# A graph layer's expert stage: results scattered in pairs of rows by node, second biases inside the products, and the full group's work between the other groups' gates

## The chip, the cores and the metric

The kernel runs on one core of a Trainium2 chip. The metric is device time in microseconds (us) of one execution; a comparison uses the median of several. A core has TensorE (PE in the profile; its weight loads are PEld), VectorE (DVE), ScalarE (ACT), GpSimd (POOL) and SyncE (SP), which mostly issues DMAs here. POOL issues the indirect DMAs, in which each of 128 partitions names the row of DRAM that it reads or writes.

## The reference

There are 3125 nodes with 512 features and 53125 edges. Two layers of graph attention and a mixing branch come first; they fill most of the time and don't change. What changes is the last step, a mixture of experts on the layer-normalized rows:

```python
logits = xf @ Wg + bg                       # 8 experts
probs = jax.nn.softmax(logits, axis=-1)
_, top_idx = jax.lax.top_k(probs, 2)
mask = jnp.any(top_idx[:, :, None] == jnp.arange(8)[None, None, :], axis=1)
comb = probs * mask.astype(probs.dtype)
for e in range(8):
    h = jax.nn.gelu(xf @ W1[e] + b1[e])     # 512 -> 128
    y = h @ W2[e] + b2[e]                   # 128 -> 512
    out = out + comb[:, e:e + 1] * y
```

The weights of the two chosen experts are not divided by their sum. All is float32.

## The kernel before

Nodes are sorted by degree and cut into 25 tiles of 128 rows (the last has 53), which stand in seven groups of four (the last has one tile). The features of a group lie transposed in SBUF as `xT`. A list scheduler orders the instructions of each engine; each engine then runs its own list strictly in that order, waiting where a semaphore says so. The tail of the program, `last`, works in stages.

**Gates** (`gates`, `in_turn`). Per group there are three passes over its tiles: transpose back to rows (L1050) and take row statistics; scale and add to `yall`, the running result (L1061, L1063), with statistics again; then normalize to `z` on ACT (L1074), store `z` to the DRAM table `zld` (L1078, on SP), transpose `z` (`to_features`, L463) and multiply with the gate weights (L1082). `in_turn` runs up to three groups at once, one pass apart. The rows of `yall` are gathered and added by POOL, tile by tile (L994, L997), the tile of 53 rows first and the full group's tiles last.

**One group is treated in full.** The tiles of group 5 (tiles 20 to 23, `ALL_EXPERTS`) go through all eight experts (`all_experts`: first products L1169, ACT's Gelu L1172, second products L1176, additions on DVE L1178). The other 21 tiles are **listed**: `choose` finds each node's two experts, `lists` sorts the node-expert pairs into 48 **parts** of 128 places, each part of one expert, and makes `which`, the rows of `zld` that a part reads, and `placei`, the two places of each node.

**Parts** (`one_expert`). POOL gathers 128 rows of `zld` (L1281), PE transposes them, multiplies with the first weights (L1288) and adds the first bias by a product of three bf16 rows (L1290: the bias cut into three bf16 pieces, against ones), ACT applies Gelu, PE transposes (L1297) and multiplies with the second weights (L1300), DVE copies (L1302), and SP stores the result to `yld` (L1303), in the order of places.

**Order of the stages.** The gates of the listed groups run first; then the first biases' bf16 rows are made (`first_biases`: POOL L1152, L1153, SP L1154, L1155); then `choose` and `lists`, with the full group's gates beside them; the full group's `second_biases` (L1139: weights of the experts, transposed, times the eight rows of biases; L1141 adds) and four of its experts' steps; the 48 parts; the other four steps. At the end, per listed tile: the second biases, two gathers from `yld` by place (L1334), two weighted additions (L1337) and a scatter to the output by node (`put`, L1158).

Buffers that matter: PSUM tags `tr` (two), `ph` (two), `py` (three) and `pg` (one); SBUF `z` (three) and `yt` (five).

Of the kernel before, what the change touches and what calls it, by code (L numbers as in the profile page):

```python
# [9 lines left out]
F32 = mybir.dt.float32  # L10
BF16 = mybir.dt.bfloat16
I32 = mybir.dt.int32
AF = mybir.ActivationFunctionType
OP = mybir.AluOpType
# [3 lines left out]
N = 3125  # L18
D = 512
# [8 lines left out]
NX = 8  # L28
# [390 lines left out]
def listed_layers(ctx: ExitStack, tc: tile.TileContext, rows,  # L419
# [581 lines left out]
    def last(xT, w1t, w2t, b2t, wgt, bgt, gt, b1t, yall):  # L1001
        with tc.tile_pool(name="fin", bufs=1, reuse_waits="tile") as fp, \
                tc.tile_pool(name="fin_p", bufs=2, space=PSUM, reuse_waits="tile") as pp:

            zld = tc.dram_tile([(NL - 1) * P + LISTED[-1][1], D], F32, name="zld")
            yld = tc.dram_tile([PARTS * P, D], F32, name="yld")

# [16 lines left out]
                           allow_small_or_imprecise_dtypes=True)  # L1024
            tiles_at = fp.tile([P, NL], F32, name="tiles_at")
            nc.gpsimd.iota(tiles_at, pattern=[[1, NL]], base=0, channel_multiplier=0,
                           allow_small_or_imprecise_dtypes=True)
            puts = []

            def gates(t0, k):  # L1030
# [6 lines left out]
                if listed:  # L1037
                    u0 = LISTED.index(tiles[0])
                    prob, rank = lprob[:, u0:u0 + k, :], lrank[:, u0:u0 + k, :]
                else:  # L1040
                    prob = fp.tile([P, GT, NX], F32, name="prob", bufs=2)
                    rank = fp.tile([P, GT, NX], F32, name="rank")
                nc.vector.memset(mv, 1.0)
                nc.vector.memset(mv2, 1.0)
                nc.vector.memset(prob, 0.0)
                yt = []
# [25 lines left out]
                for i, (t, n) in enumerate(tiles):  # L1072
                    z = fp.tile([P, D], F32, name="z", bufs=3)
                    nc.scalar.activation(z[:n], yall[:n, t, :], AF.Identity,  # L1074
                                         bias=mv2[:n, i, 0:1], scale=sd[:n, i:i + 1])
                    if listed:
                        r = (u0 + i) * P
                        nc.sync.dma_start(zld[r:r + n, :], z[:n])  # L1078
                    to_features(pp, "py", xT[:, :, t * P:t * P + n], z, n, nc.scalar.copy, bufs=3)
                    pg = pp.tile([P, NX], F32, name="pg", tag="ph", bufs=2)  # L1080
                    for c in range(NP):
                        nc.tensor.matmul(pg[:n], lhsT=xT[:, c, t * P:t * P + n], rhs=wgt[:, c, :],  # L1082
                                         start=(c == 0), stop=(c == NP - 1))
                    nc.vector.tensor_add(prob[:n, i, :], pg[:n], bgt[:n])
                    yield prob[:, :k, :], rank[:, :k, :]

            def in_turn(groups):

                running, groups, said = [], list(groups), None
                while running or groups:  # L1090
                    if groups:
                        running.append([gates(*groups[0]), groups.pop(0)[1]])

                    for i in range(GT):
                        for r in reversed(running):
                            if i < r[1]:
                                said = next(r[0])
                    for r in list(running):
                        r.append(None)
                        if len(r) == 5:  # L1100
                            running.remove(r)
                return said

# [38 lines left out]

            def first_biases():

                b1p = pp.tile([NX, FX], F32, name="b1p", tag="pg", bufs=1)
                nc.tensor.transpose(b1p, colt[:, XB1:XB1 + NX], ident)
                left = fp.tile([NX, FX], F32, name="left")
                nc.scalar.copy(left, b1p)
                b1s = fp.tile([NX, 3, FX], BF16, name="b1s")
                b1d = tc.dram_tile([NX, 3, FX], BF16, name="b1d")  # L1150
                for i in range(3):
                    nc.gpsimd.tensor_copy(b1s[:, i, :], left)  # L1152
                    nc.gpsimd.tensor_sub(left, left, b1s[:, i, :])  # L1153
                nc.sync.dma_start(b1d, b1s)  # L1154
                nc.sync.dma_start(b1t, b1d.rearrange("e i f -> i e f"))  # L1155

            def put(t, n):
                puts.append(nc.gpsimd.indirect_dma_start(  # L1158
                    out=out, out_offset=bass.IndirectOffsetOnAxis(ap=node(t), axis=0),
                    in_=yall[:n, t, :], in_offset=None))  # L1160

            def all_experts(t0, k, prob):

                gs = slice(t0 * P, min(N, (t0 + k) * P))
                w = gs.stop - gs.start
                for e in range(NX):
                    ph = pp.tile([FX, 512], F32, name="ph", bufs=2)
                    for c in range(NP):
                        nc.tensor.matmul(ph[:, :w], lhsT=w1t[:, e, c, :], rhs=xT[:, c, gs],  # L1169
                                         start=(c == 0), stop=(c == NP - 1))  # L1170
                    hT = fp.tile([FX, GT * P], F32, name="hT", tag="yt", bufs=5)
                    nc.scalar.activation(hT[:, :w], ph[:, :w], AF.Gelu_apprx_tanh,  # L1172
                                         bias=colt[:, XB1 + e:XB1 + e + 1])
                    for i, (t, n) in enumerate(TILES[t0:t0 + k]):
                        py = pp.tile([P, 512], F32, name="py", bufs=3)
                        nc.tensor.matmul(py[:n], lhsT=hT[:, i * P:i * P + n], rhs=w2t[:, e, :],  # L1176
                                         start=True, stop=True)
# [6 lines left out]
            def lists():  # L1184
# [45 lines left out]
                for o, values in ((place, both), (weight, lprob)):  # L1230
                    for i in range(2):
# [14 lines left out]
                                  for i in (0, 2, 1))  # L1246
# [5 lines left out]
                nc.scalar.activation(hots[:, :, 0, :], hot, AF.Copy, scale=number[:, 0:1])  # L1252
                nc.vector.tensor_tensor(hots[:, :, 1, :].rearrange("p (u i) q -> p u i q", i=2),
                                        hot.rearrange("p (u i) q -> p u i q", i=2),
                                        tiles_at[:, :, None, None].to_broadcast([P, NL, 2, PARTS]),
                                        OP.mult)
                pw = pp.tile([P, 2, PARTS], F32, name="pw", tag="pg", bufs=1)
                for j in range(2 * NL):
# [6 lines left out]
                nc.vector.tensor_copy(whichf, pw)  # L1265
                nc.vector.scalar_tensor_tensor(which, whichf[:, 1, :], float(P), whichf[:, 0, :],
                                               op0=OP.mult, op1=OP.add)
# [7 lines left out]
                nc.vector.tensor_copy(experti, expert)  # L1275
                return placei, weight, which, experti

            def one_expert(part, e, which):

# [19 lines left out]
                py = pp.tile([P, 512], F32, name="py", bufs=3)  # L1299
                nc.tensor.matmul(py, lhsT=h1T, rhs=w2t[:, bass.ds(e, 1), :], start=True, stop=True)  # L1300
                y1 = fp.tile([P, D], F32, name="y1", tag="z", bufs=3)
                nc.vector.tensor_copy(y1, py)  # L1302
                nc.sync.dma_start(yld[part * P:(part + 1) * P, :], y1)  # L1303


            in_turn(g for g in FGROUPS[-1:] + FGROUPS[:-1] if g not in ALL_EXPERTS)
            first_biases()
            choose(lprob, lrank)
            placei, weight, which, experti = lists()
            work = []  # L1310
            for g in ALL_EXPERTS:
                prob, rank = in_turn([g])
                choose(prob, rank)
                second_biases(*g, prob)
                work.append(all_experts(*g, prob))
            work = chain(*work)
            for _ in range(4):
                next(work)
            RB = 8
            for p0 in range(0, PARTS, RB):  # L1320
# [3 lines left out]
                for i, e in enumerate(es):  # L1324
                    one_expert(p0 + i, e, which)
            for _ in work:
                pass
            for u, (t, n) in enumerate(LISTED):
                if u % GT == 0:
                    k = min(GT, NL - u)  # L1330
                    second_biases(t, k, lprob[:, u:u + k, :])
                for i in range(2):
                    y1 = xT.tiles[4 if i else 2][:, u % 4, :]
                    nc.gpsimd.indirect_dma_start(  # L1334
                        out=y1[:n], out_offset=None, in_=yld[:, :],
                        in_offset=bass.IndirectOffsetOnAxis(ap=placei[:n, u, i:i + 1], axis=0))
                    nc.vector.scalar_tensor_tensor(yall[:n, t, :], y1[:n], weight[:n, u, i:i + 1],  # L1337
                                                   yall[:n, t, :], op0=OP.mult, op1=OP.add)
                put(t, n)
# [619 lines left out]
```

## Time and profile before

| | us |
|---|---|
| three runs: median (lowest to highest) | 2759.18 (2756.99 to 2768.11) |
| the profiled execution: time | 2757.61 |
| its span | 2755.9 |
| PE busy | 2279.7 (83%) |
| DVE busy | 1989.4 (72%) |
| POOL busy | 1482.9 (54%) |
| ACT busy | 1398.9 (51%) |
| 906 gathers of the attention (L592) on POOL | 1120.2 |
| last function, from the first gate work to the end | 2326.3 to 2755.9 |

The profile is of one execution. A row of a group gives line, engine, operation, tiles, count, busy time, mean duration in ns, and the idle time of the engine just before with what ended it. Timeline rows begin with start and duration in us. Shares of busy time are averages over stages with different limits, so the stages are read one by one. PEclk is the clock that TensorE was granted, as a share of full speed. A float32 product appears as two passes, so `x8` is four products.

### The profile page before, as it was taken

The page shows a single profiled execution, that of the slowest core. Times are in us where ns is not written, and L with a number is a line of the kernel's source. Part 1 is how long each engine was busy: PE and PEld are TensorE (multiplying, and loading weights), DVE is VectorE, ACT ScalarE, POOL GpSimd, SP SyncE. Part 2 cuts the span into 40 slices and gives each one's busy share as a digit, 9 for nine tenths or more (in the row PEclk, how much of TensorE's full clock was granted, in tenths as well). Part 3 has the DMA queues.
Part 4 walks back from the last instruction along what each step waited for, and adds up shares of the span by engine and source line. Part 5 has one row for each costly group of instructions (what it writes and reads, how often), then busy time and mean ns, then how long its engine had stood idle before and what let it go on. Part 6 is the DMA issues. An engine that isn't in the chain of part 4 may idle for free. (4 is left out here: it accounts for less than half of the span.)

```text
span 2755.9 us, 31740 instructions
## 1 busy us (share of the span) xinstructions
PE 2279.7 (83%) x9030; PEld 1302.4 (47%) x9030; DVE 1989.4 (72%) x3067; ACT 1398.9 (51%) x5365; POOL 1482.9 (54%) x1254
## 2 busy tenths in 40 slices
PE   6987988889889886999698778979897667679983
PEld 3442445555455544444344445555555343656731
DVE  6820889999999995601578988989898658664354
ACT  1111568788777773300185768776766533432200
POOL 3361778877777771011456665656667438102346
PEclk9998999989999997999799898889898868569985
DMA  8433999999989984331678878888988564214644
GB/s 283 178 118 127 341 324 330 330 338 328 338 321 344 340 308 149 131 117 76 239 253 299 317 283 314 305 321 309 320 320 285 187 185 141 71 43 124 189 132 150
DMA packets 232307, 661.88 MB, mean 240 GB/s; under 512 B 51442, under 2 KB 56951, under 8 KB 228024
## 3 DMA queue, kind: packets, MB, share of 16 engines
q0 software_dynamic: 169632, 541.48, 56.4%
q1 hardware_dynamic: 59937, 113.31, 11.3%
q10 hardware_dynamic: 2556, 4.97, 0.5%
q8 instruction: 77, 1.26, 0.2%
q14 instruction: 105, 0.86, 0.1%
HBM read 567.10 MB, written 92.69 MB: 239 GB/s over the span
## 5 line engine op out<-in xcount | busy, mean ns | idle before, releaser
L592 POOL DMA_INDIRECT lane<-kvd,idx x906 | 1120.2, 1236 | 543.0 <-issue 192.1
L633 ACT ACTIVATE lane<-lane,sc 128x64 f32<-128x64 f32 x3888 | 945.4, 339 | 113.3 <-DVE sc L623 112.9
L597 DVE TENSOR_TENSOR lane<-lane,q 128x1024 f32<-128x1024 f32 (+1 forms) x464 | 548.8, 1193 | 152.7 <-DMA lane<-kvd,idx 149.1
L653 PE MATMUL agg<-ident,lane 128*128 128x128 f32 (+1 forms) x3272 | 529.0, 301 | 139.9 <-DVE lane L636 59.4
L653 PEld LDWEIGHTS agg<-ident,lane 128*128 128x128 f32 (+1 forms) x3272 | 422.6, 154 | 314.8 <-ACT lane L633 139.5
L598 DVE TENSOR_REDUCE sc<-lane 128x16 f32<-128x1024 f32 (+1 forms) x464 | 545.3, 1187 | 2.7 <-ACT lane L633 1.7
L636 DVE TENSOR_TENSOR lane<-lane,sc 128x1024 f32<-128x1024 f32 (+1 forms) x214 | 252.3, 1197 | 0.1
L564 PE MATMUL pq<-wq,xg 128*128 128x512 f32 (+1 forms) x400 | 200.9, 632 | 17.9 <-ACT kt L743 8.5
L710 PE MATMUL po<-aT,wo 128*128 128x512 f32 (+1 forms) x448 | 198.7, 585 | 20.1 <-ACT aT L697 12.1
L1281 POOL DMA_INDIRECT xT<-zld,which x48 | 45.4, 946 | 218.5 <-DVE more L1120 116.7
L503 POOL DMA_INDIRECT kvd<-kv,rec x25 | 24.5, 980 | 223.7 <-DVE kv L500 217.7
L710 PEld LDWEIGHTS po<-aT,wo 128*128 128x128 f32 x448 | 83.3, 211 | 97.3 <-issue 65.0
L500 DVE COPY kv<-pv 128x512 f32<-128x512 f32 (+1 forms) x25 | 17.3, 692 | 153.1 <-PE pv L497 153.1
L564 PEld LDWEIGHTS pq<-wq,xg 128*128 128x128 f32 (+1 forms) x400 | 73.3, 199 | 93.5 <-issue 69.2
L381 ACT COPY kv<-pkv 128x512 f32<-128x512 f32 (+1 forms) x50 | 29.1, 585 | 163.7 <-PE pkv L379 140.1
L379 PE MATMUL pkv<-wk,xT 128*128 128x512 f32 (+1 forms) x200 | 100.7, 637 | 5.7 <-ACT kv L381 5.7
L729 PE MATMUL pq<-wmk,zT 128*128 128x512 f32 (+1 forms) x200 | 99.6, 617 | 5.6 <-ACT kt L743 3.4
L729 PE MATMUL pq<-wmp,mqT 128*128 128x512 f32 (+1 forms) x200 | 98.0, 632 | 5.3 <-ACT mqT L852 4.8
L729 PE MATMUL pq<-wmv,zT 128*128 128x512 f32 (+1 forms) x200 | 99.5, 614 | 3.2 <-DVE vt L782 2.5
L743 ACT ACTIVATE mq<-pq,hm 128x64 f32<-128x64 f32 (+1 forms) x200 | 59.3, 320 | 70.5 <-DVE hm L740 70.4
L379 PE MATMUL pkv<-wv,xT 128*128 128x512 f32 (+1 forms) x200 | 92.3, 603 | 0.0
L729 PE MATMUL pq<-wmq,zT 128*128 128x512 f32 (+1 forms) x200 | 91.4, 595 | 0.0
(339 smaller groups left out, 3275.3 us busy)
## 6 DMA issues: line engine op xcount, KB each, us to landing
lane<-kvd,idx POOLq DMA_INDIRECT x906, 6.3
kvd<-kv SPq DMA_DIRECT2D x24, 512.0 KB, 2.7
zT<-ztd SPq DMA_DIRECT2D x48, 256.0 KB, 5.9
yld<-y SPq DMA_DIRECT2D x48, 256.0 KB, 2.0
xmid<-xg SPq DMA_DIRECT2D x10, 1024.0 KB, 5.7
xT<-xmid POOLq DMA_DIRECT2D x10, 1024.0 KB, 9.5
xr<-in_x SPq DMA_DIRECT2D x24, 256.0 KB, 3.8
xb<-xo SPq DMA_DIRECT2D x24, 256.0 KB, 5.7
```

What stands on the lines that cost most here:

```text
L379: nc.tensor.matmul(ps[:n], lhsT=xT[t][:, c, :n], rhs=wkv[name][:, c, :], start=(c == 0), stop=(c == NP - 1))
L564: nc.tensor.matmul(ps[:n], lhsT=of_place(t, c), rhs=wq[:, c, :], start=(c == 0), stop=False)
L592: gets.append(nc.gpsimd.indirect_dma_start(out=kv[:n, k, :], out_offset=None, in_=kvd[l][:, :], in_offset=bass.IndirectOffsetOnAxis(ap=idx ...
L597: nc.vector.tensor_mul(ks, ks, self.q[:n, None, :].to_broadcast([n, g, D]))
L598: nc.vector.tensor_reduce(self.sc[:n, :, j:j + g].rearrange("p h g -> p g h"), ks.rearrange("p g (h d) -> p g h d", h=H), AX.X, OP.add)
L633: nc.scalar.activation(v[:, k, h, :], v[:, k, h, :], AF.Copy, scale=self.sc[:n, h, j + k:j + k + 1])
L636: nc.vector.tensor_mul(v, v, self.sc[:n, :, j:j + g].rearrange("p h g -> p g h")[:, :, :, None] .to_broadcast([n, g, H, DH]))
L653: nc.tensor.matmul(self.agg[:, c * n:(c + 1) * n], lhsT=kv[:n, k, c * 128:(c + 1) * 128], rhs=ident[:n, :n], is_transpose=True, start=firs ...
L710: nc.tensor.matmul(ps[:, :w], lhsT=wo[:, kk, c * 128:(c + 1) * 128], rhs=aT[gi][:, kk, :w], start=(kk == 0), stop=(kk == NP - 1))
L729: nc.tensor.matmul(ps[:n], lhsT=lhs(c), rhs=w[:, c, :], start=(c == 0), stop=(c == NP - 1 and bias is None))
L743: nc.scalar.activation(oh[:, h, :], ph[:, h, :], AF.Exp, bias=m[:n, h:h + 1], accum_out=s[:n, h:h + 1])
L1281: nc.gpsimd.indirect_dma_start(out=x1, out_offset=None, in_=zld[:, :], in_offset=bass.IndirectOffsetOnAxis(ap=which[:, part:part + 1], axi ...
```

## The change

- **Second biases.** `b2` is cut into three bf16 pieces as `b1` was (`biases`: three POOL copies, two subtractions, three stores and one load on SP), and each part's second product gets one more product of three rows (ones times the pieces). `second_biases` is left for the full group alone.
- **Scatter in pairs.** The result of a part goes to `yld` by an indirect DMA on POOL, to row 2 x node + choice (`goes`; places without a node go to rows of their own). A listed tile then reads both results of its nodes by one direct load on SP of 4 KB a partition. `lists` gets some small DVE steps that make `which` and `goes`.
- **Order.** The full group runs second in `in_turn`; then its `choose`, `second_biases` and one step of its experts a turn, between the gates of the other groups. What is left of the steps comes behind `lists` in the program. The order that the scheduler makes of it puts 32 of 32 first and 21 of 32 second products ahead of the last gate product.
- **Gates.** The products of a group's tiles share one PSUM buffer and one addition of the bias; the biases' bf16 rows are made behind the gates. The experts' hidden values of the full group lie in the last tile's free columns instead of a `yt` buffer.

```diff
-            zld = tc.dram_tile([(NL - 1) * P + LISTED[-1][1], D], F32, name="zld")
-            yld = tc.dram_tile([PARTS * P, D], F32, name="yld")
+            zld = tc.dram_tile([NL * P + LISTED[-1][1], D], F32, name="zld")
+            VOID = 2 * P * (NL + 1)
+            yld = tc.dram_tile([VOID + PARTS * P, D], F32, name="yld")
...
-                        r = (u0 + i) * P
+                        r = (u0 + i + 1) * P
                         nc.sync.dma_start(zld[r:r + n, :], z[:n])
+                        if u0 + i == 0:
+                            nc.sync.dma_start(zld[:n, :], z[:n])
                     to_features(pp, "py", xT[:, :, t * P:t * P + n], z, n, nc.scalar.copy, bufs=3)
-                    pg = pp.tile([P, NX], F32, name="pg", tag="ph", bufs=2)
+                    if i == 0:
+                        pg = pp.tile([P, GT, NX], F32, name="pg", bufs=1)
                     for c in range(NP):
...
-                    nc.vector.tensor_add(prob[:n, i, :], pg[:n], bgt[:n])
+                    if i == k - 1:
+                        if n < P:
+                            nc.vector.memset(prob, 0.0)
+                        nc.vector.tensor_add(prob[:n, :k, :], pg[:n, :k, :],
+                                             bgt[:n, None, :].to_broadcast([n, k, NX]))
...
+                            if r[2] in ALL_EXPERTS:
+                                prob, rank = said
+                                choose(prob, rank)
+                                second_biases(*r[2], prob)
+                                beside.append(all_experts(*r[2], prob))
+                    if beside:
+                        next(beside[0], None)
...
+                b2d = tc.dram_tile([NX, 3, D], BF16, name="b2d")
+                left = b2t
+                for i in range(3):
+                    b2p = fp.tile([P, D], F32, name="b2p", tag="yt", bufs=5)
+                    part = b2p.bitcast(BF16)[:NX, :D]
+                    nc.gpsimd.tensor_copy(part, left)
+                    nc.sync.dma_start(b2d[:, i, :], part)
+                    if i < 2:
+                        rest = fp.tile([P, D], F32, name="rest", tag="yt", bufs=5)[:NX]
+                        nc.gpsimd.tensor_sub(rest, left, part)
+                        left = rest
...
-                    hT = fp.tile([FX, GT * P], F32, name="hT", tag="yt", bufs=5)
+                    r0 = P + e % 2 * P
+                    hT = xT.tiles[-1][:, :, r0:r0 + P]
...
+                both_at = fp.tile([P, 2, PARTS], I32, name="both_at")
+                nc.vector.tensor_copy(both_at[:, 0, :], whichf[:, 1, :])
+                nc.vector.tensor_scalar(both_at[:, 1, :], both_at[:, 0, :], 1, None, op0=OP.bitwise_and)
+                nc.vector.tensor_scalar(both_at[:, 0, :], both_at[:, 0, :], 1, None,
+                                        op0=OP.logical_shift_right)
...
-                nc.tensor.matmul(py, lhsT=h1T, rhs=w2t[:, bass.ds(e, 1), :], start=True, stop=True)
+                nc.tensor.matmul(py, lhsT=h1T, rhs=w2t[:, bass.ds(e, 1), :], start=True, stop=False)
+                nc.tensor.matmul(py, lhsT=one[:, :P], rhs=b2s[:, bass.ds(e, 1), :],
+                                 start=False, stop=True)
                 y1 = fp.tile([P, D], F32, name="y1", tag="z", bufs=3)
                 nc.vector.tensor_copy(y1, py)
-                nc.sync.dma_start(yld[part * P:(part + 1) * P, :], y1)
+                results.append(nc.gpsimd.indirect_dma_start(
+                    out=yld[:, :], out_offset=bass.IndirectOffsetOnAxis(ap=goes[:, part:part + 1], axis=0),
+                    in_=y1, in_offset=None))
-            in_turn(g for g in FGROUPS[-1:] + FGROUPS[:-1] if g not in ALL_EXPERTS)
-            first_biases()
+            work = []
+            in_turn(FGROUPS[-1:] + ALL_EXPERTS + [g for g in FGROUPS[:-1] if g not in ALL_EXPERTS],
+                    work)
+            b2s = biases()
             choose(lprob, lrank)
-            placei, weight, which, experti = lists()
-            work = []
-            for g in ALL_EXPERTS:
-                prob, rank = in_turn([g])
-                choose(prob, rank)
-                second_biases(*g, prob)
-                work.append(all_experts(*g, prob))
-            work = chain(*work)
-            for _ in range(4):
-                next(work)
+            weight, which, goes, experti = lists()
+            for _ in work[0]:
+                pass
...
             for u, (t, n) in enumerate(LISTED):
-                if u % GT == 0:
-                    k = min(GT, NL - u)
-                    second_biases(t, k, lprob[:, u:u + k, :])
+                y2 = xT.tiles[(2, 0, 4)[u // 2 % 3]][:, u % 2 * 2:u % 2 * 2 + 2, :]
+                r = 2 * P * (u + 1)
+                nc.sync.dma_start(y2[:n], yld[r:r + 2 * n, :].rearrange("(r i) d -> r i d", i=2))
                 for i in range(2):
-                    y1 = xT.tiles[4 if i else 2][:, u % 4, :]
-                    nc.gpsimd.indirect_dma_start(
-                        out=y1[:n], out_offset=None, in_=yld[:, :],
-                        in_offset=bass.IndirectOffsetOnAxis(ap=placei[:n, u, i:i + 1], axis=0))
-                    nc.vector.scalar_tensor_tensor(yall[:n, t, :], y1[:n], weight[:n, u, i:i + 1],
+                    nc.vector.scalar_tensor_tensor(yall[:n, t, :], y2[:n, i, :], weight[:n, u, i:i + 1],
                                                    yall[:n, t, :], op0=OP.mult, op1=OP.add)
                 put(t, n)
```

## The prediction

> **What bounds the kernel now.** I read the chain of waits first: its pieces after 2326 us are nearly all of the last function, so I cut the profiled execution (span 2755.9, time 2757.61, so 1.7 lie around it; the median of the three runs is 2759.18, 1.6 more) into stages by busy time in windows: gates, choice and lists, a start of the experts, the experts' 48 parts, the end.
>
> ```profile
> core 0: us, PE busy (x) PEld busy (x) DVE busy (x) ACT busy (x) POOL busy (x), PEclk, DMA share, GB/s
> 2326.30:2429.30 103.00, 70.37 (x344) 63.07 (x344) 70.55 (x205) 45.18 (x82) 24.68 (x29) 0.55 0.25 82
> 2429.30:2470.50 41.20, 29.43 (x126) 19.20 (x126) 33.81 (x148) 14.98 (x19) 0.01 (x1) 0.67 0.00 1
> 2470.50:2498.70 28.20, 24.72 (x53) 10.35 (x53) 16.49 (x36) 1.86 (x3) 5.70 (x6) 0.82 0.19 56
> 2498.70:2634.90 136.20, 136.20 (x768) 96.17 (x767) 45.79 (x98) 38.01 (x94) 39.68 (x42) 1.00 0.57 173
> 2634.90:2755.90 121.00, 65.14 (x122) 23.91 (x120) 59.09 (x85) 2.75 (x4) 72.11 (x67) 0.62 0.46 145
> ```
>
> Three different limits. The gates: no engine is over 70%, the TensorE clock is granted at 0.55. The 48 parts: TensorE without a gap, 136.2/48 = 2.8 us each. The end: POOL, by the groups of 2665 to 2745:
>
> ```profile
> L1334 POOL DMA_INDIRECT xT<-yld,placei x34 | 36.7, 1080 | 10.4 <-issue 10.4
> L1337 DVE SCALAR_TENSOR_TENSOR yall<-xT,weight,yall 128x512 f32<-128x512 f32 (+1 forms) x41 | 29.9, 748 | 24.7 <-DMA xT<-yld,placei 24.5
> L1158 POOL DMA_INDIRECT out<-yall,rec x20 | 22.2, 1111 | 6.9 <-issue 4.3 <-DVE yall L1337 2.0 <-DMA out<-yall,rec 0.3
> ```
>
> POOL is busy 59 of 80 us and most of its idle time is the 0.3 us between two issues: 42 gathers and 21 puts at some 1.4 us are the end.
>
> Then the clock, from the timeline of PE in the gates and behind them:
>
> ```profile
> 2375.35 1.91 PE L463 MATMUL tr<-ident,z 128*128 128x128 f32 x8
> 2378.77 0.96 PE L1082 MATMUL pg<-wgt,xT 128*128 128x8 f32 x8
> 2411.01 3.42 PE L1082 MATMUL pg<-wgt,xT 128*128 128x8 f32 x16
> 2451.29 9.57 PE L1169 MATMUL ph<-xg,w1t 128*128 128x512 f32 x16
> 2476.22 6.72 PE L1139 MATMUL pb<-b2t,combT 8*128 8x512 f32 x8
> 2482.87 16.02 PE L1176 MATMUL py<-w2t,hT 128*128 128x512 f32 x32
> ```
>
> A tile's gate product takes 1.71 at half clock (16 passes in 3.42) and 0.96 at full. The 512-wide passes take 0.86 at half and 0.44 at full: 9.57 for 16 is a start at half and a rise after some 5 us. The second biases (8 rows) stay at half clock through 6.72 us.
>
> **The change part by part.**
>
> *Gates, +40.* The changed program's order on PE puts between the full group's last gate product and the last gate product of all: 32 first and 21 second expert products (106 passes) and 4 bias products (8 passes); 11 second products come behind. 106 x 0.44 = 47, 8 x 0.84 = 7, and some 4 us for two starts at half clock: +57 or so (58). The full group's four tiles come from the next stage: two transpose sets at 1.05 and 0.96 and a product at 1.71 are 3.7 a tile: +15. Against it: those dense products should lift the clock, and at full a tile's last transposes and gate product take 0.53 + 0.96 instead of 0.96 + 1.71. For the 20 tiles behind it 24, for 10 first transpose sets at 0.63 instead of 1.05 another 4: -28. And one stall goes:
>
> ```profile
> 2359.82 0.81 ACT L1074 ACTIVATE z<-yall,mv,sd_z 128x512 f32<-128x512 f32 x1 [7.69 <-DMA zld<-z]
> 2363.34 0.17 DVE L1084 TENSOR_TENSOR lprob<-pg,bgt 128x8 f32<-128x8 f32 x1 [8.49 <-PE pg L1082]
> ```
>
> SP held the stores of z behind the first biases' store, which waited for POOL until 2351. These now stand behind most of the gates. But the full group is now second in turn while POOL still brings its yall rows last (the last add starts at 2352.53, moved to about 2349), and DVE waits in order for it: some 4 of the 8.5 are kept. The new biases put five POOL steps and three stores into SP's queue between the stores of z of the last two groups; each waits for a yt buffer that DVE frees one tile earlier, so I cost the queued stores at nothing; if z's three buffers don't cover it, 2 to 6 us. Sum 58 + 15 - 28 - 4 = 41, taken as +40. The one gate addition for a group instead of a tile saves DVE 3 x 0.17 per group, off PE's path. Ends: +20 (clock full throughout, the other engines keep up) and +108 (below).
>
> The Trainium skill (TensorE: Matmul & The Clock Gate, Part 4: PE-mode transpose) says that transposes don't count as activity for the clock. By that the gates would fall back between the dense blocks and my -28 would be near 0, the sum near +7. The trace speaks against it: 2374.4 to 2377.1 is transposes alone, and the gate products right behind it run at 0.96.
>
> *Choice and lists, +2.* The full group's DVE work leaves this stage; 11 additions of second products enter between the choice's steps (11 x 0.67 = 7, and PE brings them each 0.88). Six more short DVE steps stand ahead of the first gather, 0.16 to 0.2 each: 1 us. Ends -5, +8.
>
> *Start of the experts, -18.* 2470.5 to 2498.7 is gather, two transposes, then 22.7 us of pb and py that the parts wait behind. These are gone; gather and transposes (6.5 us) stay, and the parts start at half clock after an idle PE, some 3.5 us. Ends -22, -12.
>
> *The 48 parts, +15.* One more product each: three bf16 rows by 512. The attention has the same one:
>
> ```profile
> 2055.09 0.39 PE L566 MATMUL pq<-bq,one 3*128 3x512 bf16 x1
> 2055.41 1.09 PE L653 MATMUL agg<-ident,lane 128*128 128x128 f32 x8
> ```
>
> 0.32 from its start to the next: 48 x 0.315 = 15, PE having no gap. POOL now issues a scatter a part beside a gather: 0.95 + 1.11 + 2 x 0.3 = 2.7 of the new 3.12 us. The scatter waits for DVE's y1 copy with a gather queued behind it; in the built order that gather stands six parts ahead of its use, and two parts' time (6 us) over its landing of 4.2 hides it. The store leaves SP. Ends +13, +35.
>
> *The end, -60.* 42 gathers become 21 direct loads on SP; 42 bias passes with their combT copies and 21 DVE additions (14 us) are gone, and so are the last four full-group experts ahead of its puts. What is left: a scatter (1.3) and its landing (3.1, as a put's); 21 puts, 21 x 1.4 = 30; DVE 42 x 0.75 = 31; and 10.7 MB read plus 5.3 written. The end's windows move 190 GB/s at a DMA share of 0.6, so 317 at a full share: 50.5 us, the largest. Behind the last data some 7 (2745.0, the last put's issue, to the end is 10.9, its landing 3). 4.5 + 50.5 + 7 = 62 against 121: -59, taken as -60, since the first six loads run without puts. Ends: -70 (DVE or POOL the bound) and -25 (loads no faster than 190 GB/s).
>
> Sum: 40 + 2 - 18 + 15 - 60 = -21: 2736.6 on the profile's scale, 2738 as a median.
>
> **The rivals.**
>
> *Half clock in the gates (slower).* If the mix of blocks and gates doesn't hold the clock, the 106 passes cost 0.86: 91, bias 7, no saving: 91 + 7 + 15 - 4 = +109, and the time is 2757.6 + 109 - 61 = 2806. It decides from a growth of 61 on. For: gates alone run at 0.55. Against: 9.57 us for 16 passes shows a rise after 5 us, and the blocks are spread over all five remaining groups.
>
> *Half the gain of the clock, or PE waiting in order for DVE's additions and its shared buffers (py, three; pg, one).* Growth 47 to 75: 2744 to 2772, no change. For: the gates' engines wait for each other now (PE 70 of 103 us). Against: expert products fill such gaps. The rule on transposes of the Trainium skill (TensorE: Matmul & The Clock Gate) would lead to this case.
>
> *POOL sets the parts' pace.* A scatter as long as the longest put (1.99) makes 0.95 + 1.99 + 0.6 = 3.54 a part: 48 x 0.42 = 20 more, 2758. For: puts in the end swing from 0.97 to 1.99. Against: the mean is 1.11.
>
> *The parts stay at half clock,* since they now start cold and the three-row product, like pb, may not count. A part is then 1.05 + 1.71 + 0.3 + 0.25 + 1.71 + 0.53 = 5.6: 48 x 2.5 = 120 more, 2858. Against: in the trace they hold 1.00 for 136 us at the same density of work.
>
> *The steps are not where the change says.* The built order shows them there; not a case.
>
> **How the numbers follow.** 0.5% (14 us) is about what a measurement of this kernel can tell from no change. Forecast (growth up to 47) 0.58; half the gain 0.16; POOL 0.08; half clock in the gates 0.13; parts at half clock 0.05. Faster is the first, 0.58; same is the second and third, 0.24; slower the last two, 0.18. The low end: gates +20, end -68, start -20, lists -3, parts +13: -58, 2700. The high end takes in the second and third cases and the beginning of the fourth: 2785. Left out: most of the half-clock cases and a rest below, under 0.2. The likeliest case's own range is 2700 to 2745.
>
> **What would show it.** Right: gates from 103 to about 143 with a granted clock over 0.75; 22 us of PE ahead of the parts gone; parts at 3.1 each, PE without gaps at 1.00; end near 61 with a DMA share near 0.9. Wrong: a clock of 0.5 to 0.6 in the gates and growth over 61; POOL busy over 95% in the parts; loads in the end one behind the other.

## The result and the profile after

The changed kernel takes 2734.73 us (median of 8 runs, 2717.68 to 2748.36), the kernel before 2760.59 (8 runs): a ratio of 0.9909, 95% interval 0.9887 to 0.9932, so it is faster by 0.9%. The forecast was 2738. Its profiled execution took 2728.12, with a span of 2726.4; it is 6.6 us below the median. The work ahead of the gates is at the same place (the graph network's last product ends at 2311.7 before, at 2311.3 after), so the stages can be laid side by side. Busy time in windows of the changed kernel, cut like those of before: gates, choice and lists, start of the experts, parts, end.

```profile
core 0: us, PE busy (x) PEld busy (x) DVE busy (x) ACT busy (x) POOL busy (x), PEclk, DMA share, GB/s
2326.30:2458.00 131.70, 109.92 (x512) 73.37 (x513) 94.58 (x247) 66.13 (x108) 28.87 (x34) 0.82 0.20 66
2458.00:2497.80 39.80, 18.62 (x68) 9.09 (x66) 36.30 (x136) 4.29 (x4) 4.05 (x4) 0.67 0.07 28
2497.80:2503.50 5.70, 1.97 (x8) 1.47 (x9) 0.00 (x0) 0.59 (x1) 4.43 (x5) 0.50 0.51 140
2503.50:2660.10 156.60, 155.30 (x810) 96.20 (x808) 44.16 (x95) 39.95 (x96) 88.33 (x91) 0.99 0.46 153
2660.10:2726.40 66.30, 0.04 (x1) 0.00 (x0) 32.13 (x43) 0.00 (x0) 24.20 (x22) 0.52 0.65 251
```

The gates grew by 28.7 us at a clock of 0.82 instead of 0.55. The start of the experts lost 22.5, the parts gained 20.4 with PE still without gaps, and the end lost 54.7: POOL is busy 24 us there instead of 72. The sum, -29.5, is the whole difference of the spans.

The end in slices of 10 us (columns as above) and its two largest groups show its new limit:

```profile
2675.00:2685.00 10.00, 0.00 (x0) 0.00 (x0) 8.40 (x12) 0.00 (x0) 6.54 (x7) 0.50 1.03 419
...
2705.00:2715.00 10.00, 0.00 (x0) 0.00 (x0) 1.91 (x3) 0.00 (x0) 1.16 (x2) 0.50 0.18 70
```

```profile
L1384 DVE SCALAR_TENSOR_TENSOR yall<-xT,weight,yall 128x512 f32<-128x512 f32 (+1 forms) x42 | 31.4, 755 | 22.2 <-DMA xT<-yld 21.3
L1196 POOL DMA_INDIRECT out<-yall,rec x21 | 23.2, 1106 | 31.0 <-DVE yall L1384 31.0
```

The transfers fill the DMA engines (a share of 1.03, 419 GB/s) up to 2705; DVE waits for loads and POOL for DVE. Then the share falls to 0.18, although one load is still out. DVE's last step in the timeline is the one that waits for it, the tile of 53 rows:

```profile
2712.98 1.52 DVE L1384 SCALAR_TENSOR_TENSOR yall<-xT,weight,yall 53x512 f32<-53x512 f32 x2 [7.55 <-DMA xT<-yld]
```

Behind it stands the last scatter to the output, issued at 2714.81. It is of 53 rows too, and the DMA view of 2714.8 to 2726.4 gives its time from issue to landing:

```profile
out<-yall,rec POOLq DMA_INDIRECT x1, 8.3
```

Most of that is its rows: from 2718.1 to 2722.7 they come in 24 packets of 4 KB (two rows each), one behind the other, at 6.3% of the 16 DMA engines, which is one engine. In the kernel before, the last scatter takes 8.2 as well.

On PE, the timeline shows gate products and transposes at full clock between the dense products, the full group's second biases (8 rows) too, and the new three-row product (L1354) in a part:

```profile
2387.72 3.70 PE L1161 MATMUL pb<-b2t,combT 8*128 8x512 f32 x8
...
2397.64 1.06 PE L1090 MATMUL pg<-wgt,xT 128*128 128x8 f32 x8
2398.55 1.10 PE L1207 MATMUL ph<-xg,w1t 128*128 128x512 f32 x2
2399.50 1.85 PE L1090 MATMUL pg<-wgt,xT 128*128 128x8 f32 x16
...
2520.58 1.12 PE L1353 MATMUL py<-w2t,xT 128*128 x2
2521.64 0.39 PE L1354 MATMUL py<-xT,one 3*128 x1
2521.96 0.33 PE L1350 MATMUL pt<-ident,xT 128*128 128x128 f32 x1
```

### The profile page after: what moved, and what is told of

Its sections match the earlier page's. It is cut to its first block, busy times and chain, and to the rows that moved or that the text cites. A ratio compares the mean times of both kernels' runs of the same rounds, so it can differ in the third digit from the quotient of the medians.

```text
span 2726.4 us, 31651 instructions
## 1 busy us (share of the span) xinstructions
PE 2229.7 (82%) x9014; PEld 1256.8 (46%) x9015; DVE 1972.5 (72%) x3024; ACT 1408.9 (52%) x5372; POOL 1499.4 (55%) x1266
## 5 line engine op out<-in xcount | busy, mean ns | idle before, releaser
L592 POOL DMA_INDIRECT lane<-kvd,idx x906 | 1133.1, 1251 | 536.0 <-issue 195.9
L653 PEld LDWEIGHTS agg<-ident,lane 128*128 128x128 f32 (+1 forms) x3272 | 417.1, 152 | 315.2 <-ACT lane L633 146.7
L502 ACT COPY kv<-pk 128x512 f32<-128x512 f32 (+1 forms) x25 | 14.6, 585 | 148.1 <-PE pk L497 148.1
```

What stands on the lines that cost most here:

```text
L592: gets.append(nc.gpsimd.indirect_dma_start(out=kv[:n, k, :], out_offset=None, in_=kvd[l][:, :], in_offset=bass.IndirectOffsetOnAxis(ap=idx ...
L653: nc.tensor.matmul(self.agg[:, c * n:(c + 1) * n], lhsT=kv[:n, k, c * 128:(c + 1) * 128], rhs=ident[:n, :n], is_transpose=True, start=firs ...
```

## Experiments

The theory was that of the prediction: the end pays for everything, by leaving POOL; the dense products cost the gates less than their length since they lift the clock; the three-row product is paid in full. Each run is read by the same stages. Here the gates are counted from the graph network's last product (15 us earlier than in the prediction) to the last gate addition of the listed groups (the full group's stands ahead of it in all but before, e2, e6, e7 and e10), the lists from there to the first gather of a part; "sum" runs to the end of the span. All in us, of one profiled execution each; the ratio is of medians to the kernel before on the same chip.

| kernel | gates | lists | to the first part | parts | end | sum | ratio (95%) |
|---|---|---|---|---|---|---|---|
| before | 117.6 | 41.2 | 28.2 | 136.2 | 121.0 | 444.2 | 1 |
| after | 146.7 | 39.8 | 5.7 | 156.6 | 66.3 | 415.1 | 0.9909 (0.9887, 0.9932) |
| e1: biases at the end | 147.8 | 42.3 | 5.8 | 137.8 | 74.6 | 408.3 | 0.9823 (0.9794, 0.9851) |
| e2: order of before | 108.5 | 37.0 | 32.6 | 155.0 | 70.3 | 403.2 | 0.983 (0.9799, 0.9862) |
| e3: gathers at the end | 145.7 | 39.8 | 5.8 | 156.5 | 106.5 | 454.4 | 1.0037 (1.0016, 1.0059) |
| e4: last load split | 147.6 | 39.8 | 5.7 | 156.1 | 58.1 | 407.3 | 0.9849 (0.981, 0.9887) |
| e5: no dense products | 148.0 | 32.8 | 5.9 | 162.6 | 67.8 | 417.1 | |
| e6: e2 + e4 | 109.6 | 37.7 | 32.9 | 160.8 | 61.4 | 402.5 | 0.9813 (0.9772, 0.9854) |
| e7: e6, experts behind | 106.3 | 36.9 | 6.0 | 162.7 | 72.1 | 384.0 | 0.9796 (0.9759, 0.9832) |
| e8: rows in turn | 143.4 | 42.4 | 5.8 | 162.7 | 66.2 | 420.4 | |
| e9: e5, no choice | 131.0 | 32.8 | 5.9 | 162.6 | 68.4 | 400.6 | |
| e10: e7, bias in copy | 108.8 | 46.1 | 5.8 | 147.2 | 75.4 | 383.3 | 0.9796 (0.9761, 0.9832) |
| e11: after again | 147.8 | 42.2 | 5.8 | 162.6 | 65.8 | 424.3 | 0.9902 (0.9865, 0.994) |

e1 to e4 shared one chip, e5 to e8 another, e9 to e11 a third. On the last two the parts of the changed kernel take 162.6 us where they took 156.6 at first. The steps of a part are as long as before; the difference is one pause of ACT, seen in all of e5 to e9 and in e11 near the 39th part (in e11 with PE waiting 3.5 us; the two steps from part to part that hold it take 11.6 us instead of 6.4):

```profile
2677.54 0.28 ACT L1348 ACTIVATE xT<-ph 128x128 f32<-128x128 f32 x1 [5.65 <-remote]
2677.87 0.48 PE L1350 MATMUL pt<-ident,xT 128*128 128x128 f32 x1 [3.48 <-ACT xT L1348]
```

What ACT waited for the profile doesn't name, so parts are compared only between runs that both have the pause or both lack it. What comes ahead of the gates differs by up to 19 us between executions on one chip (the graph network's last product ends at 2334.6 in e10 and at 2353.1 in e9), which is why single effects are read from stages and not from totals. One stage repeats within some 2 us: the gates took 145.7 to 147.8 in after, e3, e4 and e11. Laid against the changed kernel's 2734.73, the medians of e1, e2 and e4 lie 6 to 12 us below what their stages explain.

**e1: the second biases back at the end.**

```diff
-  matmul(py, lhsT=h1T, rhs=w2t[e], start=True, stop=False)
-  matmul(py, lhsT=one[:, :P], rhs=b2s[e], start=False, stop=True)
+  matmul(py, lhsT=h1T, rhs=w2t[e], start=True, stop=True)
   for u, (t, n) in enumerate(LISTED):
+      if u % GT == 0:
+          second_biases(t, k, lprob[:, u:u + k, :])
```

> The changed kernel with the second biases taken out of the parts' products and added at the end again, as before. Theory (a three-row product costs its time on a PE without gaps; the end is bound by transfers and has DVE and PE to spare): the parts go from 156.6 us to about 138 (48 x 0.385 less), the end from 66 to about 70 (DVE gets 21 additions of 0.69 and 6 copies of 0.68, in all 51 us instead of 32, and starts them 7 us before the first load lands): about 14 us less than the changed kernel, 2714 on its profile's scale. Rival (the end has nothing to spare: the bias products run at half clock there, 42 x 0.84 = 35 us, and DVE waits for each): the end grows by 18 or more and the time stays at that of the changed kernel.

Parts -18.8, or 0.39 each; end +8.3; 3.7 came back ahead of the parts: 6.8 less in all. The mechanism is as expected, the end's price about twice as large. Its windows for parts and end, columns as above:

```profile
2512.20:2650.00 137.80, 136.35 (x763) 96.22 (x763) 44.16 (x96) 39.96 (x96) 88.40 (x91) 0.98 0.53 174
2650.00:2724.60 74.60, 40.62 (x63) 13.61 (x60) 46.24 (x70) 0.00 (x0) 28.56 (x22) 0.52 0.61 224
```

DVE is busy 46 of 75 us and waits 16 us in between for bias products at half clock (0.52): the rival had that wait right and its size wrong. So second biases in the products cost some 7 us net here (10.5 by the parts and the end alone).

**e2: the full group in the order of before.**

```diff
-  in_turn(FGROUPS[-1:] + ALL_EXPERTS + others, work)
+  in_turn(FGROUPS[-1:] + others, [])
   ...
-  for _ in work[0]: pass
+  in_turn(ALL_EXPERTS, work)
+  for _ in range(3): next(work[0])
   ... parts ...
+  for _ in work[0]: pass
```

> The changed kernel with the full group's gates, choice and experts back in the order of before (gates behind the lists' start, four experts ahead of the parts, four behind). Theory (moving them between the other gates costs 29 us there and saves 24 ahead of the parts and the four experts' 28 us behind them, of which some 15 to 20 would show now that the end is short): gates 103 us, lists and start of the experts about 68 together, end about 82: 10 to 15 us more than the changed kernel. Rival (the interleaving with its higher clock is the gain of the change): the time of the kernel before, 25 or more above. Rival (the interleaving costs more than it saves): 5 us less than the changed kernel.

The theory and the first rival fell; the second had the sign, at 12 us less by stages instead of 5 (18 less by the medians, on different chips). Undoing the interleaving saves 38.2 in the gates and 4.4 in lists and parts, against 26.9 ahead of the parts and only 4.0 in the end. The four late experts hide there, where PE (27 of 70 us) and DVE (40) have room:

```profile
2308.90:2417.40 108.50, 72.07 (x354) 64.50 (x353) 84.48 (x214) 54.04 (x97) 41.57 (x46) 0.56 0.31 99
2454.40:2487.00 32.60, 30.75 (x75) 15.23 (x76) 18.66 (x50) 5.23 (x8) 7.61 (x8) 0.69 0.22 65
2642.00:2712.20 70.20, 26.74 (x60) 10.81 (x60) 40.40 (x59) 2.75 (x4) 27.76 (x26) 0.72 0.65 249
```

**e3: results stored by place and gathered at the end.**

```diff
-  results.append(nc.gpsimd.indirect_dma_start(out=yld, goes[part], in_=y1))
+  nc.sync.dma_start(yld[part * P:(part + 1) * P, :], y1)
   ...
-  nc.sync.dma_start(y2[:n], yld[r:r + 2 * n, :] ...)
+  for i in range(2): nc.gpsimd.indirect_dma_start(out=y2[:n, i, :], in_=yld, placei[:n, u, i])
```

> The changed kernel with the results stored part by part and gathered by place at the end again; biases and order as changed. Theory (the end was bound by POOL's 63 indirect transfers at 1.4 us): the end goes from 66 us to 100 to 110, with POOL busy three quarters of it, the parts stay at 156 since PE sets them; 35 to 45 us more than the changed kernel. Rival (the end became short because the biases and the full group's last experts left it): the end stays under 80, and the time within 12 us of the changed kernel.

The theory's times held: the end is 106.5, 40.2 more, and the parts are the same without the scatters (156.5), so 48 scatters cost the parts nothing. POOL is busy 64% of the end, not three quarters; with the 0.3 us ahead of nearly every issue (18.3 in all) it is 81%. Its end as a window, and POOL's gathers as a group (the wait of 22.4 began in the parts; 4 us of it lie in the end):

```profile
2664.70:2771.30 106.60, 0.08 (x1) 0.00 (x0) 32.24 (x43) 0.00 (x0) 68.45 (x63) 0.51 0.50 154
```

```profile
L1379 POOL DMA_INDIRECT xT<-yld,placei x42 | 46.2, 1100 | 34.9 <-DMA yld<-y 22.4 <-issue 12.5
```

Without this part the rest of the change makes the kernel slower than before, by 0.4% (1.0037, interval above 1).

**e4: the last load in 48 and 5 rows.**

```diff
-  nc.sync.dma_start(y2[:n], yld[r:r + 2 * n, :] ...)
+  m = n // 16 * 16
+  for a, b in ((0, m), (m, n)):
+      if a < b: nc.sync.dma_start(y2[a:b], yld[r + 2 * a:r + 2 * b, :] ...)
```

> The changed kernel with the last load, of 53 rows of 4 KB, split in 48 rows and 5. In the trace that load's rows come one behind the other at 0.16 us each, and DVE waits 7.6 us for it, while the DMA share falls to 0.2. Theory (53 rows all go through one DMA engine, 48 are spread): the wait goes, the end is 7 us shorter, 59 us. Rival (it is late as it is queued behind the 20 full loads): the end stays at 66.

The end is 8.2 shorter, and DVE's wait of 7.55 is gone; the window of the end, and DVE's last row in the timeline:

```profile
2652.30:2710.40 58.10, 0.05 (x1) 0.00 (x0) 31.82 (x43) 0.00 (x0) 24.00 (x22) 0.52 0.74 287
```

```profile
2695.57 2.97 DVE L1388 SCALAR_TENSOR_TENSOR yall<-xT,weight,yall 128x512 f32<-128x512 f32 x4 [0.81 <-DMA xT<-yld]
```

The Trainium skill (DMA: Bandwidth & Descriptors, section "Why a DMA increments its semaphore by 16 and not by 1") says that a direct copy is spread over the largest number of engines up to 16 that divides the outermost size on both of its sides; 53 is prime, so it takes one, and 48 takes 16. The 4 KB packets one at a time, 0.16 us apart, and this run agree. The last scatter is still of 53 rows: from its issue at 2698.91 to the end e4 takes 11.5 us, the changed kernel 11.6.

**e5: no expert products of the full group.** Are the gates longer by the dense products?

```diff
   for e in range(NX):
-      ... first products, Gelu, second products, additions ...
       yield
```

> The changed kernel without the full group's expert products (neither layer, nor the activation and the additions to yall; the rest stays, so the full group's rows lack their experts). From the end of the graph network's products to the last gate addition the changed kernel takes 146.7 us, and 108.5 without the full group in this stage. Theory (the dense blocks hold the clock up, gates alone run at half): the granted clock falls to about 0.56 and the stage takes 124 to 128 us (108.5 plus four tiles at 3.7 plus the waits for POOL), so 57 us of products cost some 20. Rival (the blocks only fill gaps, at whatever clock): the gate products stay at 0.12 us a pass as with the blocks and the stage falls to 112 or less.

Both were wrong. The clock falls to 0.53 as the theory said, but the stage takes 148.0, as long as with the products (145.7 to 147.8 in four executions):

```profile
2356.00:2504.00 148.00, 95.33 (x414) 81.78 (x413) 94.19 (x260) 62.72 (x109) 46.98 (x50) 0.53 0.25 80
```

Adding the products costs this stage nothing, and the lists 9.4 us beside e11 (42.2 against 32.8; 7.0 beside the first run's 39.8), by the second products and additions left over. (Without them the engines' orders are planned anew, so this is the price in a rebuilt stage, not of the same order with holes.) That doesn't mean that they only fill gaps. By the chain of waits through this stage, 71 of e5's 148.0 us lie on gate products and transposes and none on expert products; in e11, 44 and 51 of 147.8. So the products stand on the chain, and what they displace there is as long: gate products and transposes at the higher clock, and waits for the other engines.

**e9: without the full group's choice and second biases too,** beside e11, the changed kernel itself.

```diff
   if r[2] in ALL_EXPERTS:
       prob, rank = said
-      choose(prob, rank)
-      second_biases(*r[2], prob)
```

> The kernel of e5 (no expert products of the full group) also without the full group's choice and second biases; its gates stay second in turn. The stage of the gates took 148.0 us in e5, 109.6 in e6 without the full group. Theory (four tiles cost what the stage costs a tile, 109.6/21 = 5.2, so 21; the wait for POOL's rows some 3; choice and second biases the rest, 14, being 8 us of PE at half clock and two loads of ACT's tables among others): it falls to 132 to 136. Rival (the four tiles and their wait are all of the 38): it stays above 143. Rival (choice and biases, on which the other groups' steps wait in order, are most of it): 128 or less.

> The changed kernel itself, beside e9 and e10 on one chip. Every theory: about 0.991 of the time before; the stage of the gates 146 to 148 us and, at this chip's pace, the parts 156 to 163. What e9 and e10 show is held against it.

131.0, one below the theory's range: choice and second biases take 17, the four tiles with their waits 21 of the 38 us between e6 and e5. e11 repeats the result (0.9902) and the stage (147.8). The gates' window of e9, then of e11:

```profile
2353.10:2484.10 131.00, 81.00 (x402) 72.80 (x401) 88.39 (x225) 59.47 (x106) 47.14 (x50) 0.56 0.28 90
```

```profile
2351.40:2499.20 147.80, 113.21 (x520) 76.53 (x521) 108.40 (x281) 76.12 (x123) 41.56 (x46) 0.78 0.23 73
```

**e8: POOL's rows in the order of the gates.** The changed kernel's timeline of DVE has the full group waiting for rows that POOL brings last:

```profile
2345.89 0.75 DVE L1068 SCALAR_TENSOR_TENSOR yall<-yt,sd_y,yall 128x512 f32<-128x512 f32 x1 [5.94 <-POOL yall L997]
```

```diff
-  for g in FGROUPS[-1:] + FGROUPS[:-1]:
+  for g in FGROUPS[-1:] + ALL_EXPERTS + others:
```

> The changed kernel with POOL bringing the rows of yall in the order in which the gates take the groups (the full group's second instead of last). The prediction counted 4 us of waiting for these rows. Theory: the stage of the gates falls from 146.7 us by about 4, to 142 or 143. Rival (PE's first dense block waits for something else, the gates' chain through DVE and ACT): it stays within 1 us. Rival (the wait was larger than counted): it falls by 8 or more.

143.4, some 4 less than in e11 (another chip; lists and parts are as in e11) and 3 less than in the changed kernel's first run.

**e6 and e7: a better order.** If the end has room, all of the full group's work but its gates can go there.

```diff
   (e6: e2 and e4)
   (e7)
+  held = [first(e) for e in range(3)]   # first products and Gelu, in the lists
+  yield                                 # the parts come here
+  second_biases(t0, k, prob)
   for e in range(NX):
       ... second products and additions from held.pop(0) ...
+      if e + 3 < NX: held.append(first(e + 3))
       yield
```

> The kernel of e2 (full group in the order of before) with the last load split in 48 and 5 rows as in e4. Theory: the 8.5 us in which DVE waits for the last load go from the end: 70 to 62 us, 395 in all from the start of the gates, about 0.980 of the time before or less. Rival (the four experts behind the parts now pace the end): the end stays at 68 or more.

> The kernel of e6 with only the first layers of three of the full group's experts ahead of the parts (in the lists, where PE is idle); its second biases, all eight second layers and five first layers come behind the parts. Theory (PE and DVE have room in the end, none ahead of the parts): from the first gather to the first part 33 us become 7 to 10, the end grows from 62 to 68 to 76 (DVE 32 + 24 + 3 us and the last four puts): 12 to 20 us less than e6. Rival (the 46 us of products run cold and late in the end): the end grows by 25 or more, and the time stays at that of e6.

e6: the end is 61.4, as expected; the late experts don't pace it. The sum is 402.5 instead of 395, of which some 6 is ACT's pause. e7: 26.9 us gone ahead of the parts, the end longer by 10.7, 18.5 less in all by the stages of one execution each. The medians, 2746.70 and 2738.98, differ by 7.7 only, and the two intervals overlap, so the size of e7's gain over e6 stays open. DVE is now busy 54 of 72 us in the end:

```profile
2655.70:2727.80 72.10, 47.29 (x113) 20.43 (x112) 53.75 (x80) 3.44 (x5) 29.36 (x26) 0.86 0.68 243
```

**e10: the bias in DVE's copy.**

```diff
-  matmul(py, lhsT=one[:, :P], rhs=b2s[e], ...)
-  nc.vector.tensor_copy(y1, py)
+  for half, b in enumerate(b2s):        # biases held in every partition
+      nc.vector.tensor_add(y1[:, c], py[:, c], b[:, bass.ds(e, 1), :])
```

> The kernel of e7 with the second biases out of the products: DVE adds the expert's bias, held in every partition, where it copied the product to SBUF (two additions of 128x256 for a copy of 128x512), so no product of three rows is left. Theory (the parts are bound by PE alone, DVE has over 100 us idle there, and a three-row product costs 0.39 a part): the parts fall by 18 to 19 us against a kernel with them on the same chip, the rest stays: about 0.972 of the time before. Rival (DVE's longer step, and its reading of the expert's number, stands in the chain of a part): the parts fall by less than 9.

The parts fall by 15.4 against e11, less than 18 but more than the rival allows. Each has a pause of ACT in it, but of different length (PE's longest wait is 3.5 us in e11 and 1.9 in e10), so without them the gain would be some 2 us smaller. The lists grew (46.1 us instead of 36.9, with more of the full group's products in them), so the sum is that of e7, and so is the ratio: 0.9796, where 0.972 was expected. e7 and e10 beat both kernels by over 1%.

## Why the prediction was right, step by step

The forecast case came true: the gates grew by less than 47, and the end paid for it. That the median came within 3 us of the forecast is luck: the terms are off by 3 to 11 us each, in both directions, and the profiled execution's -29.5 is 8.5 more than the sum. By its own terms, in the prediction's cut:

| term | predicted | measured | which run shows it |
|---|---|---|---|
| gates | +40 | +28.7 | e2, e5, e9 |
| choice and lists | +2 | -1.4 | |
| start of the experts | -18 | -22.5 | e2, e7 |
| 48 parts | +15 | +20.4 | e1, e3 |
| end | -60 | -54.7 | e3, e4 |
| sum | -21 | -29.5 | |

*Gates: the way as forecast, 11 off in sum, wrong in make-up.* Measured from e2's stage (108.5, no stall): choice and second biases 17, four tiles and their waits 21, expert products 0, each to some 2 us; with the stall of before gone (9.1, below) that makes 29. The step that failed is "58 - 28" (7 of the 58 being bias products): the expert products and what they displace cancel in full (e5). Row by row, from before to after, the clock's gain was 24 us (gate products with xT 33.0 to 19.6, transposes of z 24.6 to 17.1, transposes back 25.2 to 21.9, the full group's in each), near the 28. The rest comes out of PE's idle time, which is 52.7 us of the stage in e5 and 34.6 in e11. The other failed step is the 3.7 us a tile: it counted PE's passes, while the stage's pace is 5.2 a tile (108.5/21). In e2 the chain of waits through this stage lies 53% on PE and some 30% on DVE, so PE's passes are about half of it. The choice's own steps and the bias products weren't counted there beyond 7 for the bias products; those ran at full clock in 3.7, against what the row at half clock had led to. That the 17 come from other groups' steps waiting in order behind them is likely but not shown. The four us of POOL's wait were right (e8). The stall in the stores of z went away altogether: in e2's gates ACT has no wait for them, and the stage is 9.1 shorter than that of before. One reading of the clock was too strong: behind the transposes of 2374.4 to 2377.1 the next eight gate passes (at 2377.09) took 1.36, and only those at 2378.77 took 0.96. The rise itself is there; the clock was granted in full from 2377.7 to 2384.6.

*Start of the experts.* The parts' first products follow the first gather at 5.7 us; the prediction kept 6.5, and 3.5 for a cold start that lies in the parts' stage instead.

*Parts.* The three-row product was taken from an attention row at 0.32 to the next start. It adds 0.39 a part (e1): 0.32 by itself, and the two passes ahead of it mostly take 1.06 to the next start instead of 0.96. The remaining 2 us are the cold start: e2, whose PE is busy ahead of the parts, takes 155.0. POOL doesn't pace the parts, with (88 us busy) or without the scatters (e3): that rival is out. Its price rested on a wrong reading: the 1.99 is a gather of yld (L1334), the longest scatter of before is 1.56, and the new ones take 0.97 to 0.98.

*End.* The cause is shown by e3: POOL's issues bounded it, and taking them away is worth 40 us of the 55. Two sizes were off and met halfway. The loads run at 419 GB/s, not 317, so the bulk ends by 2705; but "behind the last data some 7" is 21, from 2705.4, where DVE is done with the last full tile, to 2726.4. Of that, 7.6 is DVE's wait for the last load, whose rows come through one engine (e4: the end is 8.2 shorter without it), and 11.6 runs from the last scatter's issue to the end. The prediction had this second piece in hand (10.9 in before) and counted 7; its "landing 3" is the median of full scatters, while the last one took 8.2. It didn't ask how 53 rows are spread, in the load or in the scatter.

*The rivals.* Half clock in the gates: the clock was 0.82. Its mechanism is real (e5: 0.53 without the products), but the products lift the clock. What they would cost at half clock no run shows; as an estimate, e5's 95 us of PE and 106 passes at 0.86 make 186, more than the whole stage, so its price of 2806 is not refuted. Parts at half clock: 0.99. The sign of the order's move was not asked: it was priced inside the sum at +40 - 18 and the late experts inside the -60. Alone it costs some 12 us (e2), and the change would gain more without it.

## What to carry to other kernels

Price a reordering against the stage that takes the work in and the stage that it leaves: work that goes from behind a bound (here the end, the lists) into a chain of waits cost the chain's pace per tile here (5.2 us), not the passes of one engine (3.7). When a bound falls, look at what the stage has to spare next: after the gathers went, the end had PE idle and DVE idle half of the time, and leaving work there (e2, e7) brought more than moving it forward. Look at a ragged last tile by itself: its load and its scatter of 53 rows each went through one DMA engine, and splitting the load alone took 8 us off (e4).

## What was not expected of the hardware

A direct load of 53 rows of 4 KB went one row at a time, 0.16 us each, some 8 us, while the full loads of 128 rows came every 1.9 us; split as 48 and 5 the wait vanished. The last scatter of 53 rows went the same way and still does in e4; splitting it too was not tried. The load stream at the end holds 419 GB/s at a DMA share of 1.03.

TensorE's granted clock does not follow its being busy. In e5 PE works without a gap from 2448.0 to 2461.7 on transposes and 8-column gate products and stays at half speed:

```profile
2449.80 1.91 PE L463 MATMUL tr<-ident,z 128*128 128x128 f32 x8
2451.53 1.88 PE L1090 MATMUL pg<-wgt,xT 128*128 128x8 f32 x8
2453.27 1.09 PE L463 MATMUL tr<-ident,z 128*128 128x128 f32 x4
2454.15 3.42 PE L1090 MATMUL pg<-wgt,xT 128*128 128x8 f32 x16
```

Sixteen gate passes take 3.42 there and 1.85 between the dense products of the changed kernel. What share of such a mix is enough to lift the clock was not measured by itself. And ACT stood still for 5.6 us near the 39th part in every execution profiled on two chips, but for a shorter pause in e10, and in none of the other runs; what held it stays open.
